# A fixed instruction order for the convolution stages, column stores on another queue, and new slots for the last image

## The chip, the cores and the metric

The kernel runs on one core of a Trainium2 chip. The metric is the device time of one execution in microseconds (us). Five engines work side by side, each through its own queue in order: TensorE (PE in the profile; PEld is its weight load), VectorE (DVE), ScalarE (ACT), GpSimd (POOL) and SyncE (SP), which issues most of the DMA transfers. ACT can issue transfers as well.

## The reference

Two layers of a vision state-space block, each with a residual, on x of shape (8, 64, 64, 192):

```python
# per layer: K scan directions (2 in layer 0, 4 in layer 1), 384 inner channels, state 16
xz = einsum('bhwc,ec->bhwe', group_norm(x, 32), in_proj_w)      # xx and z
xc = silu(depthwise_conv_3x3(xx) + conv_b)
xs = the K readings of xc: rows, rows reversed (layer 1 also columns, columns reversed)
dts, Bs, Cs = split(einsum('bkdl,kcd->bkcl', xs, x_proj_weight))
delta = softplus(einsum(dts, dt_projs_weight) + bias)
h = exp(delta * A) * h + delta * u * B;  y = sum_n h * C         # along 4096 places
y = layer_norm(sum over directions of (y + xs * D)) * gelu(z)    # silu(z) in layer 1
x = x + einsum('bhwd,od->bhwo', y, out_proj_w)
```

All of it is float32.

## The kernel before

Each layer has two stages. **The convolution stage**, `front` (in the change's words the rounds of two chunks), goes over 8 images, each cut into 8 chunks of 512 places (8 rows of 64). Per image it loads x (`load`: four transfers for `x1`, two for `x2`), takes group statistics (`stats`, `means`, `variances`, with tiny matmuls into `pg`), normalizes x in place on ACT (`normalize`, 12 pieces), and then works in rounds of two chunks. A round projects the next two chunks (`project`: PE into `pi`, DVE copies into the padded plane `pad`), starts their tap sums (`early`: ACT writes the first tap into `tp`, L334; DVE adds four more taps, L338), and for the present two chunks runs the other four taps and the sum on PE (`conv`, into `pc`), silu on ACT into `xo` (L353), a store to `xcd`, and transposes (`turn`: PE into `px`, ACT copies into `xv`, L379, stored to `xtd`, L381). Layer 0 also forms dt, B and C here (`x_proj`, with a DVE copy to `xd`, L397). Layer 1 has instead the readings by columns: ACT copies every `xo` into `xw` with the axes swapped (L362), and after every fourth chunk three transfers store `xw` to `xcd_col` from SP's queue (L370), in rows of 128 bytes. `xv` has one buffer, the tiles of the tag `pi` have four. Inside `front` a scheduler decides the order on each engine from the order of the program and the readiness of the data; the code gives no order of its own.

**The scan stage**, `scans`, has an order written out by hand. A step is one chunk of one direction of one image: 128 steps in layer 0, 256 in layer 1. A step has 24 slots, one for each pair of states and channel tile. In a slot DVE scans (`h`, L692), POOL multiplies (`hc`, L693), PE prepares `hb` two slots ahead (L651), ACT prepares `da` four slots ahead (L668), and whatever the slot tables place there is issued between. PE sums `hc` into `py` over the step. All other matmul results (`pd`, `pb`, `pt`, `pq`, `pm`, `pz`, `po`) share one PSUM bank under the tag `m`, so that each of them waits until the one before has been read.

The output of an image (layer norm, gate, output projection, residual) comes in 8 parts of one chunk, done by the functions `f_...`. For images 0 to 6 one part goes with every K-th step (tables `L0_SLOTS`, `L1_SLOTS`). For the last image there is one part with each of the last 7 steps and one after the last scan (tables `L0_LAST`, `L1_LAST`). A part loads `xr` (x) and `yc` (y) at slot 6, takes a mean over the channels on PE (`f_mean`, L797), centers (`f_center`, L823), squares (L827), takes a second mean, makes the reciprocal deviation (`f_rstd`), scales (`f_scale`, L834), normalizes x and projects the gate (`f_norm`, `f_gate`, L780), copies it (`f_keep`, L791), applies its activation (`f_act`, L839), multiplies on POOL (`f_times`, L851), projects (`f_out`, L857), adds x (`f_add`, L866) and stores (`f_store`, L869). A slot number over 23 falls into the next step.

Of the kernel before, what the change touches and what calls it, by code (L numbers as in the profile page):

```python
# [15 lines left out]
P = 128  # L16
# [65 lines left out]
    "load": 6,  # L82
    "f_mean": (9, 17),
    "f_center": 10,
    "f_square": 10,
    "f_rstd": 18,
    "f_scale": 19,
    "f_norm": 19,
    "f_affine": 20,
    "f_gate": (20, 21, 22),  # L90
    "f_act": 23,
    "f_times": (23, 23, 24),
    "f_out": (26, 29),
}
# [31 lines left out]
    "load": 6,  # L126
    "f_mean": (11, 16),
    "f_center": 12,
    "f_square": 12,
    "f_rstd": 17,  # L130
    "f_scale": 18,
    "f_norm": 18,
    "f_affine": 19,
    "f_gate": (19, 20, 21),
    "f_act": 22,
    "f_times": (22, 22, 23),
    "f_out": (24, 28),
}
# [64 lines left out]
def front(tc, name, x_src, xcd, xcd_col, xtd, xdd, w_in, t, clear, consts):  # L203
# [7 lines left out]
    with tc.tile_pool(name=f"{name}_a1", bufs=1) as a1, tc.tile_pool(  # L211
# [50 lines left out]
        def means(b):  # L262
            im = ims[b]
            mv = a2.tile([P, 2, 2], F32, name="mv")
            nc.vector.bn_aggr(mv[:, 0], im["bst"][:, :NCH].rearrange("p c s -> p (c s)"))
            nc.vector.bn_aggr(mv[:, 1], im["bst"][:, NCH:].rearrange("p c s -> p (c s)"))
            im["pg"] = psa.tile([P, 2, 2 + CT], F32, name="pg")
            spread(im, 0, mv[:, :, 0])
# [59 lines left out]

        def early(b, c):

            tp = ims[b]["tp", c] = a2.tile([P, DT, T], F32, name="tp")
            for dt in range(DT):
                tv = tp[:, dt].rearrange("p (h w) -> p h w", w=W)
                nc.scalar.activation(tv, window(dt, c, 0), AF.Identity, scale=cw[:, dt, 0:1])  # L334
            for dt in range(DT):
                tv = tp[:, dt].rearrange("p (h w) -> p h w", w=W)
                for s in range(1, NV):
                    nc.vector.scalar_tensor_tensor(  # L338
                        tv, window(dt, c, s), cw[:, dt, s : s + 1], tv, ALU.mult, ALU.add
                    )  # L340

        def conv(b, c):
# [23 lines left out]
            if at == HC - 1:  # L366
                xwv = xcd_col[b].rearrange("(t p) (w h) -> p t w h", p=P, h=H)
                rows = slice(part * HC * RB, (part + 1) * HC * RB)
                for dt in range(DT):
                    nc.sync.dma_start(out=xwv[:, dt, :, rows], in_=xw[:, dt])  # L370

        def turn(b, c, dt):
            im = ims[b]
            if dt == 0:
                im["xv"] = a2.tile([P, T // P, D], F32, name="xv", bufs=1)
            px = psa.tile([P, T // P, P], F32, name="px", tag="pi", bufs=4)
# [9 lines left out]
        def x_proj(b, c):  # L386
# [9 lines left out]
            xd = a2.tile([P, T], F32, name="xd")  # L396
            nc.vector.tensor_copy(xd, px)  # L397
            nc.sync.dma_start(out=xdd[b][:, c * T : (c + 1) * T], in_=xd)

        load(0)  # L400
# [11 lines left out]
        nc.gpsimd.memset(pad[:, :, 1 : H + 1, W + 1 : W + 2], 0.0)  # L412
        stats(0, *range(NCH + NH))
        means(0)
        variances(0)
        normalize(0, 0)
        for dt in range(DT):
            project(0, 0, dt)
        early(0, 0)
        early(0, 1)  # L420
        normalize(0, 1, 2, 3)
        prev = None
        for g in range(B * NH):
            b, p = divmod(g, NH)
            more = b + 1 < B
            if p == 0 and more:
                load(b + 1)
            conv(b, 2 * p)
            if p == 2 and more:
                means(b + 1)  # L430
            for dt in range(DT):
                if g + 1 < B * NH:
                    project(*divmod(g + 1, NH), dt)
                if prev:
                    turn(*prev, dt)
            if prev and xdd is not None:
                x_proj(*prev)
            if p == 2 and more:
                variances(b + 1)
            if g + 1 < B * NH:  # L440
                for r in range(2):
                    early((g + 1) // NH, 2 * ((g + 1) % NH) + r)
            conv(b, 2 * p + 1)
            if p < 2 and more:
                stats(b + 1, *range(6 * p, 6 * p + 6))
            if p >= 2 and more:
                normalize(b + 1, 2 * p - 4, 2 * p - 3)
            for dt in range(DT):
                turn(b, 2 * p, dt)
            if xdd is not None:  # L450
                x_proj(b, 2 * p)
            prev = b, 2 * p + 1
        for dt in range(DT):
            turn(*prev, dt)
        if xdd is not None:
            x_proj(*prev)


def scans(tc, name, x_src, x_dst, xcd, xcd_col, xtd, xdd, t, dirs, rank, row_b, gate, slots, last, consts, dram):
# [33 lines left out]
    with tc.tile_pool(name=f"{name}_s1", bufs=1) as s1, tc.tile_pool(  # L493
# [269 lines left out]
        def f_norm(b, c):  # L763
            xn = s1.tile([P, DT, T], F32, name="xn_sq")
            fin["xn"] = xn[:CP, :CT]
# [58 lines left out]

        def f_square():
            fin["sq"] = s1.tile([P, DT, T], F32, name="xn_sq")
            nc.scalar.activation(fin["sq"], fin["y"], AF.Square)  # L827
# [107 lines left out]
        for c in range(NCH):  # L935
            b, e = B - 1, N - NCH + c + 1
            at(e, last["load"], f_load_x, b, c)
            at(e, last["load"], f_load, b, c)
# [155 lines left out]
```

## Time and profile before

| | us |
|---|---|
| median of 3 runs | 26,096.79 (26,082.51 to 26,097.9) |
| profiled execution | 26,082.78, its span 26,081.0 |
| layer 0: convolution, first to last conv matmul | 48.8 to 1,009 |
| layer 0: last scan product to first conv of layer 1 | 9,161 to 9,257 |
| layer 1: convolution | 9,257 to 10,310 |
| layer 1: last scan product to the end | 26,012 to 26,081 |

The busy time of the whole span is PE 24,246 us, DVE 24,433, POOL 22,097 and ACT 17,696; PE's mean granted clock is 0.986. A line such as `L692 DVE ...` names the line of the kernel and the engine, a wait line the waiting instruction, what released it, the total, the number of waits and the longest. Busy shares are means over stages with different limits, so the stages are read one by one.

### The profile page before, as it was taken

To read this page: it belongs to the slowest core of one execution; us is meant where nothing else is said; L and a number is where in the kernel's file an instruction comes from. 1 tells how busy PE (TensorE), PEld (TensorE's weight loads), DVE (VectorE), ACT (ScalarE), POOL (GpSimd) and SP (SyncE) were. 2 spreads that over 40 slices of the span, in tenths; PEclk is the share of its full clock that TensorE was granted. 3 is DMA by queue.
4 is the path that set the end of the run, shared out by engine and by line. 5 is a ranking of instruction groups with operands and counts; after the bars stand their busy time and mean duration, and the time that the engine had idled before them with its cause. 6 is when DMAs were issued, how large, how long until landed. Compare 5 with 4: busy or idle time off the path is not lost.

```text
span 26081.0 us, 782951 instructions
## 1 busy us (share of the span) xinstructions
PE 24246.0 (93%) x338496; PEld 13565.6 (52%) x338496; DVE 24432.7 (94%) x22459; ACT 17695.5 (68%) x27943; POOL 22097.3 (85%) x9615
## 2 busy tenths in 40 slices
PE   8899999999999877999999999999999999999998
PEld 4455555555555433555555555555555555555554
DVE  7899999999999866999999999999999999999997
ACT  4567777777777655666767767767766766766766
POOL 0399999999999700999999999999999999999997
PEclk9999999999999988999999999999999999999999
DMA  4466666666666556566575575576575575575574
GB/s 151 144 151 156 157 155 155 156 158 153 156 155 155 134 144 161 163 159 167 163 165 166 164 164 167 163 163 167 164 162 167 163 163 167 164 162 167 165 161 134
DMA packets 4225328, 4140.41 MB, mean 159 GB/s; under 512 B 2532524, under 2 KB 2732868, under 8 KB 4221892
## 3 DMA queue, kind: packets, MB, share of 16 engines
q1 hardware_dynamic: 4213744, 4083.05, 60.5%
q8 instruction: 2680, 43.91, 0.7%
q10 hardware_dynamic: 8148, 7.25, 0.1%
q14 instruction: 756, 6.19, 0.1%
HBM read 3443.63 MB, written 645.99 MB: 157 GB/s over the span
## 4 chain that ended last, share of the span: by engine, by line
DVE 25%; PE 25%; ACT 7%; issue 6%; DMA 1%; POOL 0%; SPq 0%; DVEq 0%; ACTq 0%; POOLq 0%
DVE h L692 23%; PE hb L651 10%; PE py L149 7%; PE pd L516 2%; PE pt L564 2%; ACT da L668 2%; DVE dut L614 1%; PE pz L780 1%; ACT delta L142 1%; PE pc L149 1%; PE po L857 1%; ACT L142 1%; ACT L588 1%; DMA xtd<-xv 1%; ACT delta L578 1%
## 5 line engine op out<-in xcount | busy, mean ns | idle before, releaser
L693 POOL TENSOR_TENSOR hc<-h,cr 128x1024 f32<-128x1024 f32 x9216 | 21631.9, 2368 | 3811.6 <-DMA xt_k<-xtd 2178.8
L692 DVE TENSOR_TENSOR_SCAN h<-da,st,hb 128x512 f32<-128x512 f32 x16128 | 19190.9, 1259 | 653.0 <-PE hb L651 591.7
L668 ACT ACTIVATE da<-delta,a_neg 128x512 f32<-128x512 f32 x18432 | 12143.7, 713 | 3219.2 <-DVE h L692 3213.1
L651 PEld LDWEIGHTS hb<-dg,dut 64*128 64x128 f32 x147456 | 9256.8, 186 | 7055.2 <-issue 5831.7
L651 PE MATMUL hb<-dg,dut 64*128 64x128 f32 x147456 | 10902.2, 286 | 900.6 <-DVE h L692 630.4
L149 PE MATMUL py<-hc,mask 32*32 32x512 f32 x147456 | 6877.9, 602 | 1.4 <-issue 0.8
L149 PEld LDWEIGHTS py<-hc,mask 32*32 32x32 f32 x147456 | 1570.1, 103 | 2349.4 <-issue 1768.7
L692 DVE TENSOR_TENSOR_SCAN h<-da,hb 128x512 f32<-128x512 f32 x2304 | 2611.7, 1199 | 125.7 <-PE hb L651 113.0
L698 ACT COPY st<-h 128x6 f32<-128x6 f32 x2688 | 532.6, 198 | 1854.6 <-DVE h L692 1854.1
L338 DVE SCALAR_TENSOR_TENSOR tp<-pad,cw,tp 128x512 f32<-128x512 f32 x1536 | 1086.2, 747 | 279.7 <-ACT tp L334 265.6
L564 PE MATMUL pt<-xdbl,w_dt 96*128 96x512 f32 (+1 forms) x2304 | 1299.2, 645 | 45.3 <-DVE yc L823 34.0
L606 PE MATMUL pq<-ident,delta 128*128 128x128 f32 x4608 | 760.4, 288 | 394.2 <-DVE dut L614 342.0
L578 ACT ACTIVATE delta<-pt,dtb 128x512 f32<-128x512 f32 x1152 | 782.8, 679 | 487.4 <-PE pt L564 487.4
L780 PE MATMUL pz<-xn_sq,w_in 96*128 96x512 f32 x1536 | 837.2, 645 | 17.3 <-DVE yc L834 10.8
L516 PE MATMUL pd<-x_k,w_x 128*128 128x512 f32 x1536 | 798.3, 629 | 58.5 <-ACT xv L379 28.3
L614 DVE TENSOR_TENSOR dut<-pq,xt_k 128x512 f32<-128x512 f32 x1152 | 767.2, 666 | 91.1 <-PE pq L606 91.1
L857 PE MATMUL po<-yc,w_out 128*96 128x512 f32 x1536 | 785.3, 623 | 32.7 <-POOL yc L851 25.7
L606 PEld LDWEIGHTS pq<-ident,delta 128*128 128x128 f32 x4608 | 485.1, 141 | 593.9 <-DVE dut L614 484.1
L334 ACT ACTIVATE tp<-pad,cw 128x512 f32<-128x512 f32 x384 | 264.2, 722 | 576.1 <-DVE pad L324 402.1
L149 PE MATMUL pc<-pad,taps 32*32 32x512 f32 x12288 | 598.3, 644 | 59.5 <-ACT xo L353 49.6
L851 POOL TENSOR_TENSOR yc<-yc,g 128x512 f32<-128x512 f32 x384 | 489.4, 1277 | 149.7 <-ACT g L839 113.8
L142 ACT ACTIVATE delta<-delta 128x1536 f32<-128x1536 f32 x384 | 570.5, 1486 | 4.3
(99 smaller groups left out, 10132.6 us busy)
## 6 DMA issues: line engine op xcount, KB each, us to landing
cr<-cscr SPq DMA_DIRECT2D x2048, 512.0 KB
dg<-dgd SPq DMA_DIRECT2D x1536, 512.0 KB
cr<-xdd SPq DMA_DIRECT2D x1024, 512.0 KB
xt_k<-xtd SPq DMA_DIRECT2D x768, 384.0 KB
xcd<-xo SPq DMA_DIRECT2D x128, 768.0 KB
xtd<-xv SPq DMA_DIRECT2D x128, 768.0 KB
y<-yrow SPq DMA_DIRECT2D x128, 768.0 KB
yc<-yrow SPq DMA_DIRECT2D x128, 768.0 KB
```

The source lines that it names most:

```text
L142: nc.scalar.activation(out, in_, AF.Softplus)
L149: nc.tensor.matmul(out[j * Q : (j + 1) * Q, dt], w[i * Q : (i + 1) * Q], x[i * Q : (i + 1) * Q], start=first, stop=last, tile_position=(i ...
L338: nc.vector.scalar_tensor_tensor(tv, window(dt, c, s), cw[:, dt, s : s + 1], tv, ALU.mult, ALU.add)
L516: nc.tensor.matmul(live[i]["pd"][:R], w_x[:, dt, k, :], live[i]["x"][:, dt], start=(dt == 0), stop=(dt == DT - 1),)
L564: nc.tensor.matmul(pt, w_dt[:, k, dt * P : (dt + 1) * P], live[i]["xdbl"][:rank], start=True, stop=True,)
L606: nc.tensor.transpose(pq[:, g], live[i]["delta"][:, dt, g * P : (g + 1) * P], ident)
L651: nc.tensor.matmul(hv[:, r, q], live[i]["dut"][r * G : (r + 1) * G, dt, q], dg[r * G : (r + 1) * G, q, :, 2 * mm : 2 * mm + 2], start=True ...
L668: nc.scalar.activation(da[:, n].rearrange("p (r g j) -> p r g j", r=2, j=G), live[i]["delta"][:, dt].rearrange("p (g r j) -> p r g j", r=2 ...
L692: nc.vector.tensor_tensor_scan(o, a, v, init, ALU.mult, ALU.add)
L693: nc.gpsimd.tensor_mul(hc[:, dt], h[:, dt], live[i]["cr", m])
L780: nc.tensor.matmul(fin["pz"], w_in[:, u, dt * P : (dt + 1) * P], fin["xn"][:, u], start=(u == 0), stop=(u == CT - 1),)
L857: nc.tensor.matmul(fin["po"][:CP], w_out[:, dt, u * CP : (u + 1) * CP], fin["y"][:, dt], start=(dt == 0), stop=(dt == DT - 1),)
```

## The change

The change has these parts.

- `front` writes its order out by hand in a new function `order`, under the same switch that `scans` uses. `early` becomes `first` (the ACT tap) and `second` (the DVE taps), which can be placed apart: the third channel tile of a round's second chunk is left to the next round, behind the first pad copies. `means` is split in three. Statistics of the next image come in groups of three, normalizations in groups of one or two pairs, and x of the image after next is loaded at the end of the fourth round, or of image 1 at the start.
- The stores to `xcd_col` are issued by ACT, directly behind the `xw` copies of the fourth chunk.
- In layer 0 `xv` has two buffers and the copy to `xd` moves from DVE to ACT. In layer 1 `xv` keeps one.
- The tables for the last image get new slots, with a slot for each channel tile, and the gate's products on PE come in single pieces.
- The very last part loads its x during the last step into a buffer of `xt_k` (`f_load_last`), does normalization, gate and activation ahead of the first mean, and squares into a tile `y`.

```diff
 L0_LAST = {
     "load": 6,
-    "f_mean": (9, 17),
-    "f_center": 10,
-    "f_square": 10,
-    "f_rstd": 18,
-    "f_scale": 19,
-    "f_norm": 19,
-    "f_affine": 20,
-    "f_gate": (20, 21, 22),
-    "f_act": 23,
-    "f_times": (23, 23, 24),
-    "f_out": (26, 29),
+    "f_norm": 11,
+    "f_gate": ((19, 19), (13, 13), (18, 18)),
+    "f_keep": (20, 14, 19),
+    "f_act": 20,
+    "f_mean": ((8, 8, 8), (10, 10, 10)),
+    "f_center": 9,
+    "f_square": 9,
+    "f_rstd": 11,
+    "f_scale": 12,
+    "f_affine": (18, 12, 19),
+    "f_times": (20, 20, 20),
+    "f_out": ((22, 22, 23), (26, 26, 26)),
+    "f_add": (24, 27),
 }
 L1_LAST = {
     "load": 6,
-    "f_mean": (11, 16),
-    "f_center": 12,
-    "f_square": 12,
+    "f_norm": 17,
+    "f_gate": ((20, 20), (18, 18), (21, 21)),
+    "f_keep": (21, 19, 22),
+    "f_act": 22,
+    "f_mean": ((11, 12, 12), (16, 16, 16)),
+    "f_center": 13,
+    "f_square": 16,
     "f_rstd": 17,
-    "f_scale": 18,
-    "f_norm": 18,
-    "f_affine": 19,
-    "f_gate": (19, 20, 21),
-    "f_act": 22,
-    "f_times": (22, 22, 23),
-    "f_out": (24, 28),
+    "f_scale": 17,
+    "f_affine": (19, 19, 18),
+    "f_times": (22, 22, 22),
+    "f_out": ((24, 24, 24), (28, 28, 28)),
+    "f_add": (25, 29),
 }
...
-        def early(b, c):
+        def first(b, c):

             tp = ims[b]["tp", c] = a2.tile([P, DT, T], F32, name="tp")
             for dt in range(DT):
                 tv = tp[:, dt].rearrange("p (h w) -> p h w", w=W)
                 nc.scalar.activation(tv, window(dt, c, 0), AF.Identity, scale=cw[:, dt, 0:1])
-            for dt in range(DT):
-                tv = tp[:, dt].rearrange("p (h w) -> p h w", w=W)
+
+        def second(b, c, *dts):
+            for dt in dts:
+                tv = ims[b]["tp", c][:, dt].rearrange("p (h w) -> p h w", w=W)
                 for s in range(1, NV):
                     nc.vector.scalar_tensor_tensor(
                         tv, window(dt, c, s), cw[:, dt, s : s + 1], tv, ALU.mult, ALU.add
...
                 for dt in range(DT):
-                    nc.sync.dma_start(out=xwv[:, dt, :, rows], in_=xw[:, dt])
+                    nc.scalar.dma_start(out=xwv[:, dt, :, rows], in_=xw[:, dt])
...
-                im["xv"] = a2.tile([P, T // P, D], F32, name="xv", bufs=1)
+                im["xv"] = a2.tile([P, T // P, D], F32, name="xv", bufs=1 if xdd is None else 2)
...
-            nc.vector.tensor_copy(xd, px)
+            nc.scalar.copy(xd, px)
...
+        def order():
+            stats(0, *range(NCH + NH))
+            means(0)
+            group_means(0)
+            deviations(0)
+            variances(0)
+            normalize(0, 0)
+            for dt in range(DT):
+                project(0, 0, dt)
+            for c in range(2):
+                first(0, c)
+                second(0, c, *range(DT))
+            normalize(0, 1, 2, 3)
+            if B > 1:
+                load(1)
+            prev = None
+            for g in range(B * NH):
+                b, p = divmod(g, NH)
+                more = b + 1 < B
+                n, q = divmod(g + 1, NH)
+                go = g + 1 < B * NH
+                conv(b, 2 * p)
+                for dt in range(DT):
+                    if go:
+                        project(n, q, dt)
+                    if dt == 0 and prev:
+                        second(b, 2 * p + 1, 2)
+                    if prev:
+                        turn(*prev, dt)
+                    if p == 2 and more and dt == 1:
+                        group_means(b + 1)
+                if p == 2 and more:
+                    deviations(b + 1)
+                if prev and xdd is not None:
+                    x_proj(*prev)
+                if go:
+                    first(n, 2 * q)
+                    second(n, 2 * q, *range(DT))
+                if p < 2 and more:
+                    stats(b + 1, *range(6 * p, 6 * p + 3))
+                conv(b, 2 * p + 1)
+                for dt in range(DT):
+                    turn(b, 2 * p, dt)
+                if xdd is not None:
+                    x_proj(b, 2 * p)
+                if p == 2 and more:
+                    variances(b + 1)
+                    normalize(b + 1, 0)
+                if go:
+                    first(n, 2 * q + 1)
+                    second(n, 2 * q + 1, 0, 1)
+                if p < 2 and more:
+                    stats(b + 1, *range(6 * p + 3, 6 * p + 6))
+                if p == 1 and more:
+                    means(b + 1)
+                if p == 3 and more:
+                    normalize(b + 1, 1, 2)
+                if p == 0 and b:
+                    normalize(b, 3)
+                if p == 3 and b + 2 < B:
+                    load(b + 2)
+                prev = b, 2 * p + 1
+            for dt in range(DT):
+                turn(*prev, dt)
+            if xdd is not None:
+                x_proj(*prev)
...
+        with tc.manual_schedule(engines=ENGINES):
+            order()
...
+        def f_load_last(b, c):
+            x = s1.tile([P, GC, D], F32, name="xt_k")
+            fin["late"] = x.rearrange("p g d -> p (g d)")[:CP, : CT * T].rearrange("p (u t) -> p u t", u=CT)
+            nc.sync.dma_start(
+                out=fin["late"],
+                in_=x_src[b].rearrange("(t p) l -> p t l", p=CP)[:, :, c * T : (c + 1) * T],
+            )
...
+        def f_square(end=False):
+            fin["sq"] = s1.tile([P, DT, T], F32, name="y" if end else "xn_sq")
...
+            b, e, own = B - 1, N - NCH + c + 1, last
+            if c == NCH - 1:
+                own, l = dict(last), last["load"]
+                at(N - 1, 20, f_load_last, b, c)
+                own["f_norm"], own["f_act"] = l, l + 4
+                own["f_gate"] = [(l + d, l + d) for d in range(DT)]
+                own["f_keep"] = [l + d + 1 for d in range(DT)]
+                own["f_mean"] = [[l + 5] * DT, [l + 7] * DT]
+                own["f_center"], own["f_square"], own["f_rstd"], own["f_scale"] = l + 6, l + 6, l + 8, l + 9
+                own["f_affine"], own["f_times"] = [l + 10, l + 10, l + 11], [l + 11, l + 11, l + 12]
+                own["f_out"], own["f_add"] = [[l + 12, l + 12, l + 13], [l + 15] * DT], [l + 14, l + 16]
+                at(e, l, f_load, b, c)
+            else:
+                at(e, own["load"], f_load_x, b, c)
+                at(e, own["load"], f_load, b, c)
+            at(e, own["f_norm"], f_norm, b, c)
+            for dt in range(DT):
+                thrice(e, own["f_gate"][dt], f_gate, dt)
+                at(e, own["f_keep"][dt], f_keep, dt)
             for w, (src, key) in enumerate((("y", "pm"), ("sq", "pv"))):
-                at(e, last["f_mean"][w], f_mean, src, key, 0, 1, 2)
-            for f in f_center, f_square, f_rstd, f_scale:
-                at(e, last[f.__name__], f)
-            at(e, last["f_norm"], f_norm, b, c)
-            for dt in range(DT):
-                at(e, last["f_affine"], f_affine, dt)
-                at(e, last["f_gate"][dt], f_gate, dt, 0, 1)
-                at(e, last["f_gate"][dt] + 1, f_keep, dt)
-                at(e, last["f_times"][dt], f_times, dt)
-            at(e, last["f_act"], f_act)
+                thrice(e, own["f_mean"][w], f_mean, src, key)
+            for f in f_center, f_square, f_rstd, f_scale, f_act:
+                at(e, own[f.__name__], f, *((c == NCH - 1,) if f is f_square else ()))
+            for dt in range(DT):
+                at(e, own["f_affine"][dt], f_affine, dt)
+                at(e, own["f_times"][dt], f_times, dt)
             for u in range(CT):
-                at(e, last["f_out"][u], f_out, u, 0, 1, 2)
-                at(e, last["f_out"][u] + 1, f_add, u)
-            at(e, last["f_out"][1] + 1, f_store, b, c)
+                thrice(e, own["f_out"][u], f_out, u)
+                at(e, own["f_add"][u], f_add, u)
+            at(e, max(own["f_add"]), f_store, b, c)
...
```

`thrice` issues a function once for each of three slots. The steps before the last image and all instructions inside a scan slot are as before.

More of the change, by code (lines that the diff above doesn't have):

```diff
@@ L263, in means, with group_means, deviations @@
             im = ims[b]
-            mv = a2.tile([P, 2, 2], F32, name="mv")
+            mv = im["mv"] = a2.tile([P, 2, 2], F32, name="mv")
             nc.vector.bn_aggr(mv[:, 0], im["bst"][:, :NCH].rearrange("p c s -> p (c s)"))
             nc.vector.bn_aggr(mv[:, 1], im["bst"][:, NCH:].rearrange("p c s -> p (c s)"))
+        def group_means(b):
+            im = ims[b]
             im["pg"] = psa.tile([P, 2, 2 + CT], F32, name="pg")
-            spread(im, 0, mv[:, :, 0])
+            spread(im, 0, im["mv"][:, :, 0])
+        def deviations(b):
+            im = ims[b]
+            mv = im["mv"]
             gm = im["gm"] = a2.tile([P, 2 + CT], F32, name="gm")
@@ L412, in front @@
         nc.gpsimd.memset(pad[:, :, 1 : H + 1, W + 1 : W + 2], 0.0)
[L413 to L416, printed above, removed]
-        for dt in range(DT):
[L418 to L456, printed above, removed]
+        with tc.manual_schedule(engines=ENGINES):
+            order()
 def scans(tc, name, x_src, x_dst, xcd, xcd_col, xtd, xdd, t, dirs, rank, row_b, gate, slots, last, consts, dram):
@@ L763, in f_norm @@
         def f_norm(b, c):
+            if "late" in fin and c == NCH - 1 and b == B - 1:
+                fin["x"] = fin["late"]
             xn = s1.tile([P, DT, T], F32, name="xn_sq")
@@ L823, in f_center @@
             nc.vector.tensor_sub(fin["y"], fin["y"], fin["pm"].unsqueeze(1).to_broadcast([P, DT, T]))
-        def f_square():
-            fin["sq"] = s1.tile([P, DT, T], F32, name="xn_sq")
+        def f_square(end=False):
+            fin["sq"] = s1.tile([P, DT, T], F32, name="y" if end else "xn_sq")
             nc.scalar.activation(fin["sq"], fin["y"], AF.Square)
@@ L935, in scans @@
         for c in range(NCH):
-            b, e = B - 1, N - NCH + c + 1
-            at(e, last["load"], f_load_x, b, c)
-            at(e, last["load"], f_load, b, c)
+            b, e, own = B - 1, N - NCH + c + 1, last
[13 more added lines that the diff above has]
+                at(e, own["load"], f_load, b, c)
```

## The prediction

> **What bounds the kernel now.** I read the busy time by stage first, then the waits of each stage the change touches, then the timeline around the longest of them. The columns are the stretch and its length, then busy time of PE, PEld, DVE, ACT and POOL, PE clock, DMA share, GB/s.
>
> ```profile
> 48.00:1009.00 961.00, 888.45 (x9772) 417.30 (x9771) 746.01 (x1152) 413.94 (x674) 0.00 (x0) 0.96 0.40 140
> 9257.00:10310.00 1053.00, 848.68 (x9372) 380.47 (x9371) 693.57 (x1084) 595.08 (x861) 0.00 (x0) 0.88 0.62 157
> 4600.00:5200.00 600.00, 566.71 (x8032) 333.82 (x8032) 584.51 (x512) 435.14 (x686) 559.50 (x247) 0.99 0.63 156
> 8795.05:8877.47 82.42, 70.38 (x850) 39.35 (x850) 63.59 (x56) 50.71 (x79) 60.10 (x27) 0.96 0.54 128
> 25756.03:25830.86 74.83, 70.34 (x857) 36.71 (x856) 63.88 (x56) 51.08 (x80) 60.15 (x27) 1.00 0.53 152
> 9165.00:9235.00 70.00, 38.96 (x114) 14.07 (x112) 22.71 (x38) 16.18 (x17) 4.05 (x6) 0.67 0.45 129
> 26016.00:26081.00 65.00, 34.86 (x114) 11.53 (x90) 5.56 (x5) 14.89 (x16) 3.71 (x3) 0.68 0.14 42
> ```
>
> Rows one and two are the convolution stages of layers 0 and 1. Row three, steady scans, is DVE at 97%; that code does not change. Rows four and five are one late scan step of each layer, carrying one output part of the last image: 82.4 and 74.8 us where a steady step of layer 0 takes 61.8. No engine is full in row four (PE 70.4 of 82.4). The last two rows are the ends of the layers, serial chains. So about 2,900 us can change: two stages, fourteen late steps, two ends.
>
> In layer 1's convolution stage the waits say why PE has 204 us to spare:
>
> ```profile
> DVE tp L338 <- ACT tp L334: 183.5, 41, 9.5
> ACT xv L379 <- DMA xtd<-xv: 151.8, 16, 11.4
> ...
> DVE bst L248 <- DMA x<-mid: 85.7, 18, 11.3
> ```
>
> ACT waits 16 times, twice an image, for the store of xv to land (xv has one buffer). SP's timeline shows what that store queues behind:
>
> ```profile
> 9731.93 15.89 SPq L370 DMA_DIRECT2D xcd_col<-xw  x3
> 9747.91 7.41 SPq L381 DMA_DIRECT2D xtd<-xv  x1
> 9755.42 0.47 SPq L354 DMA_DIRECT2D xcd<-xo  x1
> ```
>
> Three column stores hold SP 15.9 us (0.5, 7.1 and 8.2), the xtd store 7.4 more. Each moves 1 MB in 128-byte rows; the DMA engines are 92 to 97% busy meanwhile at some 146 GB/s, against 321 GB/s just after.
>
> **What the Trainium skill says.** "DMA: Bandwidth & Descriptors", section "Issuing engines are not separate DMA queues": queues of all issuing engines share the 16 DMA engines, and issuing elsewhere saves only the sequencer's time, "usually small relative to the DMA itself". The sharing is not shown here; the issue is not small (15.9 us). Its specifications ask for 512 bytes or more at line rate: the trace agrees (146 against 321 GB/s). "TensorE: Matmul & The Clock Gate", "What's actually happening", has TensorE at half clock after about 3.4 us idle. The trace agrees: six pm records take 2.81 us in a busy step of layer 1 and 4.28 in a waiting one of layer 0; four pz records 1.98 in a step, 3.78 at the end.
>
> **The change part by part.**
>
> *Layer 0's convolution.* A steady round of two chunks keeps PE full: conv 4.86, turn and x_proj 4.04, conv 4.85, three projects with turns 10.94, x_proj 2.67, together 27.36. Four rounds and the two pg groups (1.72 + 1.84) make 113.0 an image; the stage takes 960/8 = 120. The 7 us go at image boundaries: twelve normalizations in one block on ACT (8.56 us), statistics on DVE waiting for x (32.3 us in the stage). The change loads x a round ahead (six SP issues) and spreads both. PE's order in a round stays. On DVE I lay out: tap sums of the first chunk 12 x 0.665 = 8.0 after PE's x_proj, three statistics 1.9, eight sums 5.3, three statistics 1.9, then the pad copy PE needs: 1.1 us late in the two rounds with statistics, hidden otherwise. Image 115.2: seven boundaries x 4.8 = 34 less; start 4 more. xd goes to ACT (64 x 0.6 us), hidden: ACT is busy 414 of 961. **-30** (bounds -50 and 0).
>
> *Layer 1's convolution.* xv keeps one buffer here. SP loses the 16 groups of column stores, so the 11 us xv waits go. But ACT now issues them, between xw and xv, and I take ACT to be held 15.9 us each time. The trace has no large ACT-issued store under back-pressure, but shows compute standing behind ACT's DMA issues:
>
> ```profile
> 9244.61 0.44 ACTq L166 DMA_DIRECT2D a_neg<-l_A_logs  x1
> 9245.10 2.22 ACT L289 ACTIVATE x<-x,gnb,grs 128x512 f32<-128x512 f32 x3 [6.99 <-DMA w_x<-l_x_proj]
> ```
>
> Behind it stand xv (three copies), the next tp starts, then xo; for those wait DVE's tap sums, behind them in DVE's order the pad copies, and for them PE's projects. Chain from conv to conv, durations from ACT's and DVE's timelines: xo 1.8, xw 3.1, [stores 15.9], xv 1.6, first tp 0.7, eight sums 5.3, [statistics, means], to the pad copies; then pads 1.3, four sums 2.7, pad 0.65, project 2.1, turn 0.5, conv 4.86 = 12.1. Rounds: 40.5 (stores), 26.5 (one batch of statistics, 1.9), 43.0 (stores, statistics, means 2.5), 28.8 (square root, its table load and normalizations, 4.2): **138.8 us an image**, and some 2 for the half clock after each 15 us hold, against 1053/8 = 131.6. 8 x 9.2 = 74, less 9 for the last image, which prepares no successor: **+65**. Bounds: not held -190 (16 x 15.9 = 254 less); held longer, rival below.
>
> *Late steps, layer 0.* Each of seven has some 18 us of DVE waits in its timeline. The first is 5.2: the mean stands at slot 9 while y's load, issued at 8862.67, lands at 8868.9; SP held that issue because the load of xr, ahead of it, waited for the store of the part before. The second is 5.5: the second mean, slot 17, needs the one PSUM bank "m", which make_dut of the same slot frees, and PE has nothing else for the scans. The change adds the outputs at 24 and 27 instead of 27 and 30, so the store leaves ahead of y; puts both means at 8 and 10, rstd 11, scale 12; spreads gates over 13, 18, 19. Slot by slot with PE's pieces (hb 1.1, py 2.2, mean 2.8 warm, gate 1.9, po 2.8) I get about 72 us, little above PE's 67.4 (70.4 less 3 for warm means). What is late next is hb behind the two means, 2 to 4 us. 7 x 10.4 = **-73** (bounds -95 and 0).
>
> *Late steps, layer 1.* PE has 70.3 of 74.8; its order hardly changes: gate and mean slots move by one or two, the three products lie together, one 2.4 us hc less ahead of the last. 1.3 a step, 7 steps: **-9** (+10 to -25).
>
> *Ends.* After the last scan, y is stored, waits for an xr store and load, is loaded; two means, then normalization, three gates, activation, product. The gates with activation stand after the scale, from 26050.1 to 26066.2, half clock. The new order loads x during the last step (one SP issue into an idle xt_k buffer) and puts normalization, gates and activation ahead of the mean, over y's store and load. That takes 15 us off each chain and 2 to 4 of xr's wait; but y's mean now stands behind three gates on PE (8 us warm, 13 at half clock, after y's copy), which gives back up to 3: **-18 and -14**, bounds -5 and -22 each.
>
> Scans between do not change; the new slots lie on the last image alone.
>
> **Sum:** -30 + 65 - 73 - 9 - 32 = -79. The profiled execution took 26,082.8 (span 26,081.0), which makes 26,004; the median of the three runs, 26,096.8, is 14 higher, so 26,018. 0.2% is 52 us, about what a measurement of this kernel can tell from no change.
>
> **Rivals.**
>
> *ACT is not held.* If ACT's queue takes the three stores at the 0.5 us of the first, layer 1's stage loses 254 more: 25,764. For: 0.5 us when nothing is outstanding. Against: second and third wait until the one before drains, and three always come together. 0.15.
>
> *Slower: two queues share the engines.* If xcd and xtd stores and the next image's loads on SP's queue run while column stores drain, those get half the rate and ACT is held 29 us instead of 15.9: 16 x 13 = +210, 26,228. It decides from 24 us a hold (131/16 above 15.9). For: engines already 92 to 97% busy. Against: SP has one 768 KB store ready then (2.4 us at 321 GB/s); the next xtd store, and the loads behind it, wait for ACT itself. 0.16.
>
> *Late steps stay as they are.* y's mean stands a slot earlier and may only move the wait; PE may be the limit already: 82 us lost, 26,100. For: PE 94% in layer 1's steps. Against: layer 0's 82.4 with the same PE time. 0.14.
>
> Forecast 0.55.
>
> **Numbers.** Forecast alone: 25,940 to 26,090. The range 25,800 to 26,150 adds the third rival and the near parts of the others; it leaves out half of the first and most of the second. Faster: 0.44 + 0.15 + 0.02 = 0.61. Same: 0.10 + 0.10 + 0.01 = 0.21. Slower: 0.01 + 0.02 + 0.15 = 0.18.
>
> **What would show it.** Column-store issues on ACT of 7 to 8 us; layer 1's stage near 1,118 us with no xv wait on xtd; layer 0's near 930; late steps of layer 0 near 72 us, of layer 1 above 73; each end some 15 shorter. Wrong if ACT's issues are all near 0.5 us, if they exceed 12, or if late steps stay at 82.

## The result, and the profile after

The kernel after takes **26,104.73 us** (12 runs, 26,096.02 to 26,122.06) against 26,093.46 before (12 runs on the same chip): ratio 1.0006, 95% interval 0.9997 to 1.0015. That is no change that this measurement can tell. The likeliest case of the prediction, 26,018, did not come. The profiled execution took 26,096.3 (span 26,094.5), 13.5 us more than the profiled one of before. So some 2,900 us of the kernel were rebuilt and nothing came out at the end. The stages show why: gains and a loss of some 80 us, and one large gain that did not happen.

The first view is the busy time by stage of the kernel after, its rows in the order of those shown of before (stretch, length, then PE, PEld, DVE, ACT, POOL, PE clock, DMA share, GB/s).

```profile
48.00:998.00 950.00, 888.83 (x9768) 418.52 (x9768) 739.64 (x1103) 455.21 (x742) 0.00 (x0) 0.98 0.40 142
9214.00:10349.00 1135.00, 807.85 (x9396) 380.00 (x9392) 742.10 (x1103) 604.98 (x869) 0.00 (x0) 0.84 0.57 146
4600.00:5200.00 600.00, 566.30 (x8030) 334.01 (x8030) 583.06 (x512) 427.96 (x679) 558.53 (x247) 0.99 0.65 153
8769.91:8852.42 82.51, 72.18 (x851) 40.13 (x850) 63.82 (x56) 51.02 (x79) 59.86 (x28) 0.92 0.53 127
25794.30:25868.39 74.09, 70.31 (x860) 36.70 (x858) 63.95 (x56) 51.23 (x80) 60.09 (x27) 1.00 0.54 152
9143.00:9192.00 49.00, 27.87 (x86) 10.68 (x80) 13.47 (x22) 13.61 (x15) 3.71 (x3) 0.78 0.63 177
26050.00:26094.50 44.50, 25.92 (x90) 8.56 (x70) 5.56 (x5) 13.61 (x15) 3.70 (x3) 0.83 0.17 53
```

Layer 0's convolution is 10 us shorter, layer 1's 82 longer, with no engine busy for more than 808 of its 1,135 us and PE's granted clock down from 0.88 to 0.84. The steady scans are as before. A late step of layer 0 still takes 82.5 us. Both ends are some 25 us shorter. From the boundaries of the stages (last conv matmul, last scan product, first conv, last store):

| stretch | predicted | measured |
|---|---|---|
| layer 0, convolution | -30 | -10 |
| layer 1, convolution | +65 | +82 |
| layer 0, late steps | -73 | about 0 (all of layer 0's scans: -8) |
| layer 1, late steps | -9 | -5 (all of layer 1's scans: -2) |
| ends of layers 0 and 1 | -18, -14 | -25, -24 |
| sum | -79 | +13 |

The waits of layer 1's convolution in the kernel after (total, number, longest):

```profile
DVE tp L351 <- ACT tp L345: 240.9, 44, 16.0
...
ACT xv L392 <- issue: 212.9, 15, 14.7
...
ACT xv L392 <- DMA xtd<-xv: 8.2, 12, 0.9
```

The 16 waits for the store of xv are gone (151.8 us before, 8.2 now). In their place are 15 stretches of 14 us in which ACT waits for nothing that the profile shows. The timeline of ACT shows one of them:

```profile
9638.70 0.52 ACTq L383 DMA_DIRECT2D xcd_col<-xw  x1
9639.57 1.15 ACT L375 COPY xw<-xo 128x512 f32<-128x512 f32 x1
9639.73 14.91 ACTq L383 DMA_DIRECT2D xcd_col<-xw  x2
...
9654.73 1.56 ACT L392 COPY xv<-px 128x512 f32<-128x512 f32 x3 [14.01 <-issue]
9656.17 1.97 ACT L345 ACTIVATE tp<-pad,cw 128x512 f32<-128x512 f32 x3
```

ACT's own queue issues the second and third column store for 14.91 us, and once the copy of xw is through, no other instruction of ACT runs meanwhile. The first taps start behind them at 9656.17, and DVE has then stood for 15.6 us. This is the hold that the prediction argued from a few short issues.

The late step of layer 0, in the timeline of SP, PE and DVE around the loads of the output part:

```profile
8828.61 0.81 SPq L784 DMA_DIRECT2D yrow<-y  x2
...
8833.31 0.48 SPq L795 DMA_DIRECT2D xr<-x  x1
8833.88 0.40 SPq L809 DMA_DIRECT2D yc<-yrow  x1
...
8841.69 4.80 PE L847 MATMUL pm<-yc,mean_w 128*128 128x512 f32 x6 [5.25 <-DMA yc<-yrow]
...
8846.53 1.75 DVE L873 TENSOR_TENSOR yc<-yc,pm 128x1536 f32<-128x1536 f32 x1 [6.75 <-PE pm L847]
```

The load of xr no longer holds SP: y is loaded 5.3 us after its store was issued, where it was 11.05 before. But PE has come to the mean, now at slot 8, at 8836.4, and y lands at 8841.7. PE stands 5.25 us and then computes the mean largely at half speed (4.80 us; the second mean of the step, six like matmuls, takes 2.84). DVE's next instruction is the centering, which needs the mean, and it stands 6.75.

### The profile page after: what moved, and what is told of

It is laid out like the page before. It is cut to its first block, busy times and chain, and to the rows that moved or that the text cites. A ratio compares the mean times of both kernels' runs of the same rounds, so it can differ in the third digit from the quotient of the medians.

```text
span 26094.5 us, 783031 instructions
## 1 busy us (share of the span) xinstructions
PE 24180.9 (93%) x338496; PEld 13548.6 (52%) x338496; DVE 24456.7 (94%) x22395; ACT 17739.3 (68%) x28006; POOL 22094.2 (85%) x9615
## 4 chain that ended last, share of the span: by engine, by line
PE 41%; DVE 38%; ACT 10%; issue 9%; DMA 1%; ACTq 1%; POOL 0%; DVEq 0%; SPq 0%; POOLq 0%
DVE h L731 33%; PE hb L690 17%; PE py L153 11%; ACT da L707 3%; PE pt L603 2%; PE pz L830 2%; PE pd L555 2%; PE po L907 2%; DVE tp L351 2%; DVE dut L653 1%; ACT delta L146 1%; PE pc L153 1%; ACT L146 1%; ACT L627 1%; PE pi L320 1%
## 5 line engine op out<-in xcount | busy, mean ns | idle before, releaser
L320 PE MATMUL pi<-x,w_x 128*128 128x512 f32 x768 | 444.1, 688 | 376.8 <-ACT x L300 135.1
L392 ACT COPY xv<-px 128x512 f32<-128x512 f32 x384 | 212.3, 598 | 748.7 <-PE px L391 477.3
```

## The experiments

The times of stages are read from the profiled runs, first to last conv matmul; a late step is the mean distance between the same product of successive steps. For reference: layer 0's stage 959 before and 949 after, layer 1's 1,052 and 1,134, late steps of layer 0 82.8 and 83.1.

### Layer 1: the column stores on SP, and on POOL

```diff
-                    nc.scalar.dma_start(out=xwv[:, dt, :, rows], in_=xw[:, dt])
+                    nc.sync.dma_start(out=xwv[:, dt, :, rows], in_=xw[:, dt])
```

> The kernel after, with the three column stores issued by SP again; nothing else moved. If ACT's standing still is what the fixed order pays in layer 1's convolution: the 15 waits of xv that end with no releaser (212.9 us) go, the stage falls from 1,134 us, but the next xtd store stands behind 15.9 us of stores on SP, so that xv waits some 8 to 10 us after each store: stage 1,020 to 1,060. If instead the fixed order of rounds itself is what costs (pad copies and sums in a worse order), the stage stays at 1,110 to 1,140. Layer 0 and the scans stay as after.

Measured: stage 1,047 us, total 26,014.13, ratio to before 0.9972 (0.9961 to 0.9983). ACT's standing still is what the stage pays: the issuing queue alone is worth 87 us. The waits of the stage show what takes its place.

```profile
ACT xv L392 <- DMA xtd<-xv: 256.9, 20, 18.0
```

The wait for the store of xv is back, and at 12.8 us each it is longer than I expected.

The same line with `nc.gpsimd` in place of `nc.sync`:

> The kernel after, with the three column stores issued by POOL, which has nothing to do in this stage. If only the issuing engine's standing still costs, neither ACT nor SP stands still and layer 1's convolution falls to the chain without the hold, (138.8 - 2 x 15.9) x 8 = 856, with start and end 870 to 910 us; total some 25,850. If the column stores take the DMA engines from the other transfers (xtd stores, x loads), the stage ends at 960 to 1,050 with waits on xtd or x. If POOL's own issue is slower than SP's (no large store of POOL's is in the trace), the stores pile up and xw's buffers hold ACT: 1,050 or more.

Measured: stage 1,016 us, total 26,001.71, ratio 0.9968 (0.9955 to 0.9981). It is the middle theory: neither ACT nor SP stands, but xv still waits 117.7 us for xtd stores, which are under way beside the column stores. The instructions of the line (nanoseconds, minimum, median, maximum) in this kernel, and one group of three in POOL's timeline:

```profile
L383 POOL DMA_DIRECT2D xcd_col<-xw x48: 2717/2718/2846, 9281.6 to 10275.9; - x48
```

```profile
9547.67 2.72 POOL L383 DMA_DIRECT2D xcd_col<-xw  x1 [24.61 <-ACT xw L375]
9564.09 2.72 POOL L383 DMA_DIRECT2D xcd_col<-xw  x1 [13.70 <-ACT xv L392]
9576.77 2.72 POOL L383 DMA_DIRECT2D xcd_col<-xw  x1 [9.96 <-ACT tp L345]
```

The issue itself takes 2.7 us each time. But POOL is held too, between its issues: in every group the second and third store start 12.7 to 20.4 us after the one before, 0.3 us after it has landed (from issue to landing a store takes 16.2 us, median). The ACT instructions in the brackets are not what POOL waited for. POOL has nothing else to do in this stage, so its standing costs nothing.

### Is it the order or the queue? The old order with the stores on ACT

The kernel before, with `nc.scalar` in place of `nc.sync` in its L370.

> The kernel before (order by the scheduler), with the three column stores issued by ACT and nothing else changed. If ACT's standing still costs whatever the order, layer 1's stage, 1,053 us before, grows by about as much as in the fixed order (1,134 on ACT against 1,047 on SP, +87): 1,120 to 1,160. If the fixed order is what makes the hold costly, the stage stays within 30 us of 1,053.

Measured: stage 1,126 us (+74), total 26,167.17 in one run, and the same 15 stretches of ACT (212.8 us). The hold costs 74 us in the scheduler's order and 87 in the fixed one. The fixed order alone, with the stores on SP, makes 5 us in this stage (1,052 to 1,047), which is less than its spread: with the stage unchanged from after, five other kernels below took 1,129 to 1,139.

### What makes the hold: the same bytes in long rows

```diff
-                xwv = xcd_col[b].rearrange("(t p) (w h) -> p t w h", p=P, h=H)
-                rows = slice(part * HC * RB, (part + 1) * HC * RB)
+                n = W * HC * RB
+                xwv = xcd_col[b].rearrange("(t p) l -> p t l", p=P)
                 for dt in range(DT):
-                    nc.scalar.dma_start(out=xwv[:, dt, :, rows], in_=xw[:, dt])
+                    nc.scalar.dma_start(
+                        out=xwv[:, dt, part * n : (part + 1) * n],
+                        in_=xw[:, dt].rearrange("p w h -> p (w h)"),
+                    )
```

> The kernel after, with the column stores on ACT writing the same megabyte in rows of 8 KB instead of 128 bytes: xcd_col then holds its elements in another order, so layer 1's column scans run on permuted data. If ACT is held because a store must drain at the 146 GB/s of 128-byte rows, the hold falls from 15 us to 0.5 + two stores at about 320 GB/s = 7 us, and the stage from 1,134 to about 1,134 - 16 x 8 = 1,006 (980 to 1,030). If the hold is a cost of issuing from ACT whatever the rows, it stays at 15 us and the stage at 1,134.

Measured: stage 960 us, total 25,911.56 (one run). The instructions of the store's line in this kernel, and in the kernel after:

```profile
L383 ACTq DMA_DIRECT2D xcd_col<-xw x48: 326/401/1857, 9266.5 to 10172.6; - x48
```

```profile
L383 ACTq DMA_DIRECT2D xcd_col<-xw x48: 520/7169/10219, 9273.8 to 10363.6; - x48
```

Both theories missed. The hold is gone altogether, not halved: 0.4 us a store with the same megabyte. It follows the rows, not the bytes; their length and their number changed together, so these runs do not part the two. The DMA view of the stage counts 369,360 packets for 45 of ACT's stores in short rows, 8,208 each, and 6,480 in long ones, 144 each. The Trainium skill, "DMA: Bandwidth & Descriptors", section "Why a DMA increments its semaphore by 16 and not by 1", says that one descriptor moves one contiguous run of the last dimension; 1 MB in 128-byte runs is 8,192 of them, in 8 KB runs 128, and the counts agree but for 16 more a store. The same page's section "Issuing engines are not separate DMA queues" calls the sequencer's time for an issue usually small. For the long rows that holds (0.4 us); for the short ones the measurement decides (7.2).

The long rows issued by POOL:

> The same long rows (xcd_col in another order), issued by POOL. With 128-byte rows POOL's stage took 1,016 us and not 870 to 910. If the DMA engines' time in short rows makes up the rest (xtd stores and x loads behind them: 117.7 us of xv waits), the stage falls to 880 to 930. If the chain of the fixed order itself is longer than my 107 us an image, the stage stays above 960.

Measured: stage 954 us, total 25,910.37 (one run), between the two theories. In long rows POOL issues the three stores of a group 1.0 us apart, before the first has landed. With POOL issuing, the short rows cost 62 us of the stage (1,016 to 954). Likely they do so through the DMA engines that they occupy: the column stores take 12.4% of the engines' time here and 30.6% in short rows, and xv's wait for xtd stores falls from 117.7 to 32.1 us. The rest, 954 against the 880 to 930 of my chain, belongs to the order: with no hold anywhere the round chain takes 122.8 us an image (first group product to the next in the long-row kernel on ACT, steady images), where the prediction had 107.

### Layer 0: the first tap ahead of xd

```diff
-                if prev and xdd is not None:
-                    x_proj(*prev)
                 if go:
                     first(n, 2 * q)
+                if prev and xdd is not None:
+                    x_proj(*prev)
+                if go:
                     second(n, 2 * q, *range(DT))
```

> The kernel after, with the first tap on ACT ahead of the copy of xd, so that it no longer waits for x_proj on PE; layer 0 alone has xd. DVE's sums wait for the first tap 110.6 us in 37 waits, 3 us each. If that is what makes DVE late for the pad copies in the rounds with statistics, those two rounds lose 2.5 us or more each of their 4 and 7.8 us: image 121.2 to 114-117 us, stage 950 to 915-925. If the statistics on DVE are the cause by themselves, the stage moves by less than 10 us. Layer 1 stays as after.

Measured: stage 915 us (949 after), an image 116.1 us (121.2 after), total 26,073.96, ratio 0.9994 (0.9985 to 1.0002). This timeline of the kernel after shows what was in the way:

```profile
465.15 2.74 PE L402 MATMUL px<-xo,w_x 128*128 128x512 f32 x6
465.35 0.59 ACT L392 COPY xv<-px 128x512 f32<-128x512 f32 x1 [3.52 <-PE px L391]
...
467.97 0.58 ACT L410 COPY xd<-px 128x512 f32<-128x512 f32 x1 [2.04 <-PE px L402]
468.45 1.94 ACT L345 ACTIVATE tp<-pad,cw 128x512 f32<-128x512 f32 x3
...
469.21 1.54 DVE L351 SCALAR_TENSOR_TENSOR tp<-pad,cw,tp 128x512 f32<-128x512 f32 x2 [3.17 <-ACT tp L345]
```

ACT has little to do, but it waits for PE's x_proj to copy `xd`, and the first tap stands behind that copy. DVE loses some 3 us (3.17 here) in every round, also in the two that the statistics delay, where it has none to spare: in after those two took 31.1 and 34.9 us (30.3 and 33.3 in every other image), the shortest round 27.1. Of the 34.9, some 3.6 are the two pg groups, which belong there. PE's waits for the pad copies in this stage, after and then with the edit:

```profile
PE pi L320 <- DVE pad L335: 58.1, 41, 2.9
```

```profile
PE pi L320 <- DVE pad L335: 33.9, 43, 2.5
```

### Late steps of layer 0: is it y?

```diff
-                at(e, own["load"], f_load_x, b, c)
-                at(e, own["load"], f_load, b, c)
+                if xdd is not None:
+                    at(e, 4, f_load_other, b, c)
+                    at(e, own["load"], f_load_x, b, c)
+                else:
+                    at(e, own["load"], f_load_x, b, c)
+                    at(e, own["load"], f_load, b, c)
```

`f_load_other` reads a chunk of `xcd` in place of y.

> The kernel after, but in the first seven output parts of layer 0's last image the load of y reads a chunk of xcd (as large, written long before) and stands at slot 4, ahead of the load of xr: the output of these parts is wrong, and the load waits for no store. If the wait of the first mean for y (PE stands 5.2 us, DVE 6.8) is what keeps the step at 82.5 us, a step takes 72 to 75. If the wait only hides another limit (two means three slots apart, PE's clock, the bank m), a step stays at 79 or more.

Measured: 74.4 us a step, total 26,034.15 (one run). The wait for y is the stall. PE's waits over the late steps of the kernel after have this line, and those of the edited kernel none:

```profile
PE pm L847 <- DMA yc<-yrow: 37.2, 6, 6.9
```

A real repair has to move the mean behind the landing (in this diff and the next, lines of the table are joined, and entries that move along with these are left out):

```diff
-    "f_norm": 11, "f_gate": ((19, 19), (13, 13), (18, 18)), "f_keep": (20, 14, 19),
-    "f_mean": ((8, 8, 8), (10, 10, 10)), "f_center": 9, "f_square": 9, "f_rstd": 11, "f_scale": 12,
+    "f_norm": 15, "f_gate": ((19, 19), (17, 17), (18, 18)), "f_keep": (20, 18, 19),
+    "f_mean": ((11, 11, 11), (13, 13, 13)), "f_center": 12, "f_square": 12, "f_rstd": 14, "f_scale": 14,
```

> The kernel after, with the two means of layer 0's last image at slots 11 and 13 instead of 8 and 10, and centre, square, rstd, scale, norm and gates behind them; outputs stay at 22 and 26. A step was 83.1 us in after and 74.4 with a y that waits for no store. If y's landing (12 us after its store is issued, 5.2 after PE is ready at slot 8) is the whole stall, three slots of 2.4 us cover it and a step takes 74 to 76. If the plan with means so late only moves the stall to the second mean, the gates or the outputs (bank m), a step takes 78 to 83.

Measured: 80.3 us a step, total 26,086.93, ratio 0.9999 (0.9990 to 1.0008). PE's wait for y is all but gone:

```profile
PE pm L847 <- DMA yc<-yrow: 2.3, 2, 1.4
```

But the step gains 2.8 us only. POOL now waits 2.7, 3.9 and 6.2 us for h later in the step, and behind the last of these DVE waits 6.1 to 6.3 us for hb: the second theory. I took the 6.2 us, behind three close gates, for the cause, and spread them.

```diff
-    "load": 6,            "f_gate": ((19, 19), (17, 17), (18, 18)), "f_out": ((22, 22, 23), (26, 26, 26)),
+    "load": 6, "load_x": 8, "f_gate": ((21, 21), (17, 17), (19, 19)), "f_out": ((26, 26, 26), (29, 29, 29)),
```

> The kernel after, with another table for layer 0's last image: means at 11 and 13 as in the trial before, gates apart at 17, 19 and 21, outputs at 26 and 29 in the slots where PE has least to do, and the load of xr at slot 8, behind the load of y, so that it holds y back no more. If bunching on PE (three gates in slots 17 to 19 behind the bank m, a 6.2 us stall of DVE) is what the trial with later means still paid over 74.4, a step takes 75 to 77 us instead of 79.5. If the second mean with pq and dut around it (2.7 + 3.9 us) is the larger part, it stays at 78 to 80.

Measured: 80.5 us a step, total 26,091.09 (one run). That was a miss, so I tried the gates alone: the kernel that loads y from elsewhere, with its means left at 8 and 10, and norm and gates at 15 and 17 to 19.

> The trial with y read from a chunk of xcd (the first seven output parts of layer 0's last image then use other data), means at 8 and 10 as there, but the normalization at 15 and the three gates at 17, 18 and 19 as in the trial with later means. The first took 74.4 us a step, the second 79.5. If the gates standing close behind dut of slot 17 on the one bank m are what the later means paid, a step takes 78 to 80 here too. If the means at 11 and 13 between dut of slots 13 and 15 are, it stays at 74 to 75.5.

Measured: 75.1 us a step (74.4 without), total 26,043.79 (one run). The gates cost some 1 us. That leaves the place of the later means: at 11 and 13 they lie between the three products `pq` of slots 12, 14 and 15, all in the one bank m, and each has to be read by another engine before the next starts. This is by elimination, and the waits at `pq` do not show it: PE stands 2.0 us a step there with the later means, and 2.0 in this trial as well. What the traces do show is PE's speed. Its first gate in such a step and the sum behind it, with the later means and then in this trial:

```profile
8941.55 3.75 PE L830 MATMUL pz<-xn_sq,w_in 96*128 96x512 f32 x4 [1.73 <-DVE dut L653]
8945.23 3.53 PE L153 MATMUL py<-hc,mask 32*32 32x512 f32 x48
```

```profile
8917.59 1.96 PE L834 MATMUL pz<-xn_sq,w_in 96*128 96x512 f32 x4 [1.73 <-DVE dut L653]
8919.47 2.21 PE L153 MATMUL py<-hc,mask 32*32 32x512 f32 x48
```

The two take 3.1 us more with the later means, and by as much DVE's wait for hb behind them is longer (6.2 us against 3.1). The clock granted to PE over five late steps is 0.94 in both trials with later means and 0.98 in both with y from elsewhere. So some 3 of the 5 us between them are PE's speed; why it drops when the means stand later was not tested.

### Two versions with the repairs

The first joins `first` ahead of `xd`, the table with the gates spread, and an `xcd_col` whose rows hold the two halves of the columns one after the other (shortened in the diff). ACT stores 8 KB rows as above, and a column scan loads its chunk (and the first direction its y) in two pieces of 1 KB a row; nothing is left out.

```diff
+        def by_parts(i, tl):                     # n = L // 2, m = T // 2
+            for q in range(2):
+                nc.sync.dma_start(out=tl[:, :, q * m : (q + 1) * m],
+                    in_=tiles(xcd_col[b])[:, :, q * n + c * m : q * n + (c + 1) * m])
+            return tl.rearrange("p t (q w h) -> p t w q h", w=RB, h=HC * RB)
```

> The kernel after with three edits together: first tap ahead of the copy of xd (layer 0's stage 915 us), that table for layer 0's last image (steps 75 to 79), and xcd_col laid out so that ACT's column stores write rows of 8 KB while a column scan's load of a chunk takes two pieces of 1 KB a row (layer 1's stage 960). If the stages add, 26,104.7 - 34 - 174 - 7 x 5 = 25,862, ratio to before 0.991. If the loads in two pieces make layer 1's column scans wait for x, part of it is given back: above 25,900.

Measured: 25,879.73 us, ratio **0.9921** (0.9908 to 0.9935). Stages: layer 0 915, layer 1 957, late steps 81. The stages add: the 18 us over the expected sum are the late steps, 81 and not 78. The loads in two pieces cost the scans nothing that shows.

The second takes the slots of after for gates and outputs, puts the means at 9 and 11, and gets y out earlier.

```diff
-    "keep_y": 29,      # layer 0, every step
+    "keep_y": 27,
-    "load": 6,
-    "f_mean": ((8, 8, 8), (10, 10, 10)), "f_center": 9, "f_square": 9, "f_norm": 11, "f_rstd": 11,
+    "load": 4, "load_x": 6,
+    "f_mean": ((9, 9, 9), (11, 11, 11)), "f_center": 10, "f_square": 10, "f_norm": 12, "f_rstd": 12,
```

> The best version so far (first tap ahead of xd, column stores in long rows) with yet another layer-0 end: gates, norm and outputs at the slots of after, means at 9 and 11, y copied out two slots earlier in every step of layer 0 (slot 27), loaded at slot 4, and xr loaded behind it at 6. If y's landing is the stall, y comes 5 us sooner and the mean one slot later, which covers the 5.2 us wait: late steps of layer 0 at 74 to 76 us, and the total falls from 25,879.7 by 7 x 5 = 35 to some 25,845. If copying y out earlier makes the steady steps wait (one copy a step, 256 steps), the scans lose more than that: above 25,880.

Measured: 25,891.13 us, ratio 0.9925 (0.9911 to 0.9938), no better than the first. Late steps take 73.1 us, nearly all that the prediction had promised, with PE's clock at 1.00, and the rival of this run came true as well. The busy time of two milliseconds of steady scans, first version and then this one:

```profile
3000.00:5000.00 2000.00, 1888.56 (x26688) 1111.42 (x26687) 1937.06 (x1696) 1432.55 (x2256) 1860.69 (x816) 0.99 0.64 156
```

```profile
3000.00:5000.00 2000.00, 1879.97 (x26402) 1108.40 (x26401) 1918.40 (x1680) 1421.05 (x2237) 1844.02 (x809) 0.98 0.64 154
```

DVE gets through 1% less work in the same time (1918.40 against 1937.06). Over some 7,500 us of steady steps that is 73 us (an estimate), more than the 7 x 7.5 = 53 that the late steps gained (80.6 to 73.1). Layer 0's scans agree: they took 17 us longer in all. The earlier copy in the last image's steps alone was not tried.

## Why the prediction was right or wrong

**The case that came** is the third rival, late steps that stay (26,100), to which the prediction gave 0.14, and for the reason that it gave: y's mean stands earlier and only moves the wait. The total lies in the range of 25,800 to 26,150 because that was widened for this rival; the forecast alone, 25,940 to 26,090, missed it. That the rival's figure fits to 5 us is luck: the two convolution stages came out 37 us worse than it assumes, the ends 17 and the scans 10 better.

**Layer 0's late steps (-73, measured about 0).** Right: the store leaves ahead of y, and y's load goes out earlier. Right too: with y at hand a step takes 73 to 74 us (74.4 and 73.1 in two runs). The step that failed is the placing of y itself: I wrote that both means stand at 8 and 10 and laid out PE's pieces from there, without asking when y lands. Before, y landed 17.3 us after its store was issued. Without the hold for xr (11.05 - 5.3 us) that falls to 11.6 (13.1 measured), and PE comes to slot 8 after 7.8. The issue and landing of y's load that I quoted lie 6.2 us apart; set beside the slots, they would have told it. The wait moved forward with the mean and did not shrink.

**Layer 0's convolution (-30, measured -10).** The layout of DVE's round was right, 115.2 us an image against 116.1 once its assumption is true. The step that failed is "hidden: ACT is busy 414 of 961", said of the copy to xd. ACT had the time, but in order: the copy waits for x_proj, and the first taps wait for the copy. I priced a moved instruction by its duration and not by what it makes its queue wait for, though I did so for layer 1.

**Layer 1's convolution (+65, measured +82).** The mechanism was right: stores of 7.2 us, ACT held 14.9 us instead of 15.9, the xv waits gone, the stage longer. Two terms of the sum were mis-sized and partly cancelled, so that +65 came near to +82 in part by luck: the chain without holds is 122.8 us an image, not 107.0, and a hold adds (146.1 - 122.8) / 2 = 11.7 us, not 15.9, although the 11.7 include what the short rows cost besides ACT's standing. Why a hold of 14.9 us adds less was not tested; part of it may lie beside waits that are there anyway. The layout had missed waits that the long-row kernel shows: PE's projects stand 65.9 us in that stage for pad copies behind the statistics, and 48.9 for xv copies behind xw. My figure for the bound "not held", 863 us, was too low for the same reason: 954 to 960.

**Rivals.** "ACT is not held": refuted by the issues of 7.2 us. The reason against it, that a store waits until the one before drains, was seen for POOL in short rows; in long rows it fails, where POOL started three within 2.1 us and ACT took 0.4 us for one. "Two queues share the engines": the hold stayed at 14.9, far from the 24 from which it decides. The reason given, that SP has little to send then, was not tested. What sharing there may be shows where no engine with work of its own is held: 62 us with POOL issuing.

**Ends (-32, measured -49).** From the copy of y to the last store the chains shrank by 18.5 and 19.0 us, where I had 18 and 14. The other 6.1 and 5.3 us I had not counted: the previous part's gates and outputs leave PE earlier, so that y is copied 2.0 us after the last product instead of 8.1 and 7.3. **Layer 1's late steps** (-9, measured -5) were right in kind and small.

## What to carry to other kernels

Price a DMA issue by its rows: one that took 0.4 us in long rows held its engine for 7 us in short ones, and moving it to another queue only changes who stands still; change the layout on both sides instead. When an instruction moves to an idle engine, write down what it waits for and what stands behind it there. When an order is moved forward, look up when each input lands, and put its first reader behind that.

## What the runs showed of the hardware

- A store of 1 MB held ACT 7.2 us (median) in 128-byte rows and 0.4 in 8 KB rows; the first of three in short rows took 0.5 us even so. Whether the length or the number of the rows sets the hold, and how, stays open.
- POOL issued the same short-row store in 2.7 us each time, and the long-row one in 0.53. The short-row store landed 16.2 us (median) after its issue, and POOL started the next of a group only when it had; the long-row one landed after 8.1, with up to three under way.
- The DMA view counts 8,208 packets for a short-row store from ACT, and some 272 for the same store from POOL (12,510 for 46).
- PE was slower after some waits: the six matmuls of a mean took 4.80 us after 5.25 us of standing, and 2.84 for the second mean of the same step; a gate's four took 3.75 or 1.96 behind the same wait of 1.73.
